# Cross-attention block in fp32: scores, G and h regrouped by quads of four tiles

## The chip, the cores and the metric

The kernel runs on one core of one Trainium2 chip. The metric is the device time of one execution in microseconds (us). All arithmetic is fp32. The engines are TensorE (matmuls; PE in the profile, its weight loads PEld), VectorE (DVE), ScalarE (ACT), GpSimd (POOL) and SyncE (SP), which issues all the DMAs here. Matmul results land in PSUM, which has eight banks of 128 partitions x 512 fp32 values.

## The reference

```python
text_p  = einsum('bld,dh->blh', x, W_text) + b_text            # x: (4, 2048, 512)
audio_p = einsum('bsd,dh->bsh', ctx_768, W_audio) + b_audio    # ctx_768: (4, 77, 384)
Q = layer_norm(text_p, g1, beta1)
K = layer_norm(audio_p, g2, beta2)
V = audio_p
alpha   = softmax(einsum('blh,bsh->bls', Q, K) / sqrt(512))    # 77 keys
H_hyper = einsum('bls,bsh->blh', alpha, V)
H_hyper = einsum('blh,hk->blk', H_hyper, W_out) + b_out
return layer_norm(H_hyper + x, g_out, beta_out)                # (4, 2048, 512)
```

## The kernel before

The 8192 rows of x are cut into 64 tiles of 128 rows, 16 tiles to each of the four batches; a group of four tiles is loaded at once. Instead of projecting x and normalising it, the kernel folds the projection into two small matrices made once in a prologue (the first 37 us). **Scores**: Q K^T is x times a 512 x 77 matrix per batch (made at L340, 78 columns with one for the offset), later scaled by 1/std of the row. **Variance**: the sum of squares of the projected row is the quadratic form x G x^T, where G = W W^T of the centred weights is a 512 x 512 matrix (made at L645). G is symmetric, so only a triangle of its 32-column blocks is kept, the off-diagonal ones doubled (`gram_out`). **Values**: V W_out + b_out is made once as `vw`, so that one matmul with softmax weights gives h.

For each tile, in order:

- `turn` (step x): VectorE transposes a 128 x 512 tile of x into `xt`, in 32 x 32 blocks; the DMA that loads `xq` has put the blocks in the right place.
- `project_chunks` (steps p and P): four matmuls, one for each 128 rows k of the contraction, with `xt[:, k]` as the 128-column stationary operand. The moving operand `mu` holds score columns and G columns side by side, in four parts of `SQ` = 20 score columns and up to 96 G columns: 464, 464, 336 and 208 columns for k = 3, 2, 1, 0 (L452). The last 128 G columns, which only k = 3 needs, don't fit the bank and go as a matmul of their own to another bank, `yl` (L460).
- `score_last` and `score` (t, s): VectorE adds the offsets to the scores, and multiplies the G product by x and sums it along the row, in two instructions (L476), one for each bank. The row sums go to `ss`.
- `row_scale` (r): GpSimd turns `ss` into 1/std. `scale_scores` (c): VectorE scales the scores and takes the row maximum. `exponential` (e): ScalarE.
- `turn_weights` (w, W): TensorE transposes a tile's 128 x 77 weights (L535), and ScalarE copies the result out of the bank (L536).
- `apply` (a): one matmul with 77 rows and 512 columns gives h (L543). `residual` (z): VectorE multiplies by 1/sum, adds x and sums the row. `squares` (q), `minus_mean` (n), `deviations` (d), `norm_shift` (o), `norm_on_scalar` (y), `norm_on_gpsimd` (m) make the last layer norm, over ScalarE and GpSimd; every fourth tile or so takes `norm_on_vector` (v, V) instead. `store` writes the tile.

The small steps (r, c, e, ...) are shared by a batch of tiles: four tiles, and two or one for the last 16 tiles (`LAST`). The order of all instructions on every engine is the program's: the first 40 tiles follow a loop with fixed distances between the steps, the rest a list written out step by step (a letter for the step, a number for the tile). `in_program_order` pins it. Every engine works its own queue in order; a DMA on SP's queue that has to wait holds up those behind it.

PSUM: banks h (two), y (two), yl0, yl1, prep, gain. In the prologue they serve as scratch; in the loop yl0 and yl1 take G's last columns and the transposed weights, prep and gain hold two constants that are read in place of SBUF (`keep`). vw is made in three blocks (L382) between the first tiles, and two of the four batches' vw are put together by DMAs.

## Time and profile before

| what | us |
|---|---|
| median of two runs | 293.35 (293.11 and 293.58) |
| span of the profiled execution | 291.9 |
| VectorE: L556 residual, L476 products of 384 and 128 columns, L403 transpose, mean of one | 0.733, 0.626, 0.353, 0.704 |
| ScalarE: L609 scale and shift, L564 squares, L523 exponential, mean of one | 0.802, 0.718, 0.349 |
| GpSimd: L613 gain, L614 shift, mean of one | 1.272, 1.271 |
| GpSimd: L506 clamp and L212 power of a four-tile batch, mean of one | 0.227, 1.037 |
| DMA: 55.33 MB in all, mean rate | 190 GB/s |

Rows of the profile name line, engine, operation, output <- inputs by tile names, shapes and count. In the lists of groups the numbers behind the bar are total busy time in us and the mean of one in ns, then the engine's idle time just before them. In a timeline a row begins with its start in us from the beginning of the span and its length; equal neighbours are merged (x2, x6). Records of matmuls overlap, since the end of one is modelled and the next starts streaming before: the distance from start to start is the cost of one, not its length.

### The profile page before, as it was taken

What the parts mean: (1) busy time and instruction counts of PE and PEld (TensorE: products, weight loads), DVE (VectorE), ACT (ScalarE), POOL (GpSimd) and SP (SyncE); (2) the same over time, 40 slices, a digit from 0 to 9 for tenths busy, and PEclk for the clock granted to TensorE, in tenths of its full rate; (3) what the DMA queues carried; (4) which work ended last, traced back from release to release, by engine and by line L of the source; (5) the groups of instructions that cost most, each with busy time, mean ns of one, the idle gap of its engine ahead of it and who ended that gap; (6) DMA issues with size and microseconds to landing.
All of it is one profiled execution on the core that took longest, in us unless ns stands there. A gap on an engine that the chain in (4) does not pass through costs nothing.

```text
span 291.9 us, 4021 instructions
## 1 busy us (share of the span) xinstructions
PE 283.0 (97%) x1034; PEld 171.6 (59%) x1034; DVE 227.1 (78%) x715; ACT 153.3 (53%) x486; POOL 157.2 (54%) x168
## 2 busy tenths in 40 slices
PE   8999999999999999999999999999999999999990
PEld 7786755565555555555555555556555556555540
DVE  1586133586878888888888989898999999989995
ACT  2646210031446383838383838366967767477571
POOL 1022000011026576757676767687989878977833
PEclk9999999999999999999999999999999999999996
DMA  6899913359390967887777878789689887612214
GB/s 200 212 267 370 214 65 99 61 183 249 92 227 36 186 245 161 274 171 263 167 265 165 269 162 270 160 274 206 262 174 294 200 270 204 159 72 88 108 58 180
DMA packets 54178, 55.33 MB, mean 190 GB/s; under 512 B 2597, under 2 KB 35697, under 8 KB 54155
## 3 DMA queue, kind: packets, MB, share of 16 engines
q1 hardware_dynamic: 54155, 55.07, 70.0%
q8 instruction: 8, 0.13, 0.2%
q14 instruction: 15, 0.12, 0.2%
HBM read 37.97 MB, written 16.78 MB: 188 GB/s over the span
## 4 chain that ended last, share of the span: by engine, by line
PE 94%; DVE 3%; issue 1%; DVEq 0%; ACT 0%
PE y L452 53%; PE h L543 18%; PE yl L460 5%; PE vw_ps L382 4%; PE m_ps L340 3%; PE vat_ps L264 3%; PE et_ps L535 2%; PE w_ps_yl L645 2%; PE w_ps_yl L208 1%; PE w_ps_y L645 1%; DVE z L595 1%; PE uw_ps L358 1%; DVE z L556 1%; DVE y L593 1%; PE va_ps L284 0%
## 5 line engine op out<-in xcount | busy, mean ns | idle before, releaser
L452 PE MATMUL y<-mu,xt 128*128 128x464 f32 (+2 forms) x512 | 179.6, 473 | 0.0
L452 PEld LDWEIGHTS y<-mu,xt 128*128 128x128 f32 x512 | 89.7, 190 | 49.6 <-issue 32.3
L543 PE MATMUL h<-vw,et 77*128 77x512 f32 x128 | 64.1, 594 | 0.1
L564 ACT ACTIVATE sqj<-z,sz 128x512 f32<-128x512 f32 x64 | 46.0, 718 | 31.9 <-DVE z L556 31.0
L613 POOL TENSOR_TENSOR z<-z,go 128x512 f32<-128x512 f32 x44 | 56.0, 1272 | 10.0 <-ACT z L609 9.4
L614 POOL TENSOR_TENSOR z<-z,beo 128x512 f32<-128x512 f32 x44 | 55.9, 1271 | 3.5
L556 DVE SCALAR_TENSOR_TENSOR z<-h,inv,x 128x512 f32<-128x512 f32 x64 | 46.5, 733 | 2.3 <-PE h L543 1.7
L403 DVE STREAM_TRANSPOSE xt<-xq 128x512 f32<-128x512 f32 x64 | 44.7, 704 | 0.5 <-PE y L452 0.5
L476 DVE CUSTOM_DVE_ANT_1 yl<-yl,x,bc 128x128 f32<-128x128 f32 x64 | 22.6, 353 | 28.2 <-PE yl L460 28.1
L476 DVE CUSTOM_DVE_ANT_1 y<-y,x,e 128x384 f32<-128x384 f32 x64 | 40.1, 626 | 2.3
L506 POOL TENSOR_SCALAR rs<-ss 128x4 f32<-128x4 f32 (+2 forms) x21 | 4.7, 223 | 66.9 <-DVE ss L476 66.6
L460 PEld LDWEIGHTS yl<-ub,xt 128*128 128x128 f32 x128 | 23.6, 188 | 26.2 <-issue 15.6
L609 ACT ACTIVATE z<-z,no,ro 128x512 f32<-128x512 f32 x44 | 34.5, 802 | 0.1
L536 ACT COPY et<-et_ps 77x256 f32<-77x256 f32 (+1 forms) x33 | 11.9, 361 | 39.5 <-PE et_ps L535 39.5
L212 POOL TENSOR_TENSOR ro<-ro,mhalf 128x4 f32<-128x4 f32 (+2 forms) x21 | 18.2, 867 | 23.7 <-ACT ro L576 23.6
L523 ACT ACTIVATE e<-e,mx 128x77 f32<-128x77 f32 x64 | 22.2, 349 | 11.9 <-DVE mx L516 11.9
L543 PEld LDWEIGHTS h<-vw,et 77*128 77x128 f32 x128 | 23.3, 190 | 7.0 <-issue 5.2
L460 PE MATMUL yl<-ub,xt 128*128 128x128 f32 x128 | 24.5, 273 | 0.0
L212 POOL TENSOR_TENSOR rs<-rs,mhalf 128x4 f32<-128x4 f32 (+2 forms) x21 | 18.6, 886 | 1.8
L498 DVE TENSOR_TENSOR e<-y,uws 128x80 f32<-128x80 f32 x64 | 15.0, 234 | 4.6 <-PE y L452 3.4
L535 PEld LDWEIGHTS et_ps<-ident,e 128*77 128x77 f32 x64 | 9.4, 147 | 15.1 <-issue 10.7
L593 DVE SCALAR_TENSOR_TENSOR y<-z,nm,gain_ps 128x512 f32<-128x512 f32 x20 | 14.9, 752 | 0.8
(107 smaller groups left out, 254.5 us busy)
## 6 DMA issues: line engine op xcount, KB each, us to landing
xq<-in_x_dram SPq DMA_DIRECT2D x64, 256.0 KB, 4.9
x<-in_x_dram SPq DMA_DIRECT2D x16, 1024.0 KB, 6.1
out_dram<-z SPq DMA_DIRECT2D x64, 256.0 KB, 2.5
wc<-in_L_xattn_W_text_dram SPq DMA_DIRECT2D x4, 256.0 KB, 5.2
wo<-in_L_xattn_W_out_dram SPq DMA_DIRECT2D x1, 1024.0 KB
wa<-in_L_xattn_W_audio_dram SPq DMA_DIRECT2D x3, 256.0 KB, 3.6
rows<-in_L_xattn_b_text_dram SPq DMA_DIRECT2D x1, 256.0 KB
bo<-in_L_xattn_b_out_dram SPq DMA_DIRECT2D x1, 256.0 KB
```

Source lines behind the costliest of these rows:

```text
L212: nc.gpsimd.tensor_tensor(dst, v, mhalf[: v.shape[0], : v.shape[1]], ALU.pow)
L403: nc.vector.transpose(xt.rearrange("p k (a j) -> p a k j", j=R), xq[i][:, t].rearrange("p a (k i) -> p a k i", i=R),)
L452: nc.tensor.matmul(parts(y[:, : Q * AQ])[:, :, cols], lhsT=xt[:, k, :], rhs=mub[:, k, :, cols], start=(k == LAST_K), stop=(k == 0),)
L460: nc.tensor.matmul(b, lhsT=xt[:, k, :], rhs=ub.rearrange("p q i -> p (q i)"), start=True, stop=True)
L476: nc.vector.tensor_tensor_reduce(out=y, in0=y, in1=x, scale=1.0, scalar=first, op0=ALU.mult, op1=ALU.add, accum_out=to)
L523: nc.scalar.activation(e, e, AF.Exp, bias=s.mx[:, c], accum_out=s.inv[:, c])
L543: nc.tensor.matmul(s.h[n], lhsT=s.et[:, n - s.tiles[0], :], rhs=s.vw, start=True, stop=True)
L556: nc.vector.scalar_tensor_tensor(z, s.h.pop(n), s.inv[:, c], xs[i][:, t, :], ALU.mult, ALU.add, accum_out=s.sz[:, c])
L564: nc.scalar.activation(junk, s.z[n], AF.Square, bias=s.sz[:, c], scale=-float(H), accum_out=s.sq[:, c])
L609: nc.scalar.activation(z, z, AF.Identity, bias=s.no[:, c], scale=s.ro[:, c])
L613: nc.gpsimd.tensor_tensor(z, z, go, ALU.mult)
L614: nc.gpsimd.tensor_tensor(z, z, beo, ALU.add)
```

## The change

Tiles are handled by quads of four (14 quads, then batches of 2, 2, 2, 1 and 1 tiles).

- **G fills a bank** (`form`, step G): the moving operand is G alone, 512, 384, 256 and 128 columns for k = 3 to 0, in one y bank; `form_sum` (s) is one VectorE instruction over 512 columns. yl's own matmul is gone.
- **Scores in their own bank** (`score`, step S): four matmuls of 78 columns for each tile, with the same stationary operands as G; the four tiles of a quad share one bank (yl0 and yl1 by turns). `offsets` (A) adds the offsets of a whole quad in one instruction.
- **Keys in three pieces**: `exponential` writes the 77 weights of a row (padded to 96 with zeros) as three pieces of 32, the pieces of the four tiles side by side; so a transpose of 128 x 128 (three for a quad) puts the four tiles' weights on the four groups of 32 partitions.
- **h of four tiles in row groups of 32 rows** (`apply_four`, step H): for each piece four matmuls, one per tile, each with 32 rows (13 in the last piece) of its own group of partitions, 512 columns, to four different banks (h, h, prep, gain), accumulated over the three pieces. vw is made by pieces too (W, U) and copied by 19 DMAs to all four groups of partitions; the last eight tiles keep the matmul of 77 rows.
- The transposed weights use the scores' bank; `keep` keeps one constant, late. `deviations` is split into two steps (d, D), `norm_on_gpsimd` into m and M, `norm_shift` goes from ScalarE to VectorE. 57 tiles end on GpSimd, 7 on VectorE. The loop is replaced by a list of steps for all tiles; matmuls that only kept TensorE warm near the end are gone.

```diff
-    soft = ctx.enter_context(tc.tile_pool(name="soft", bufs=4))
+    soft = ctx.enter_context(tc.tile_pool(name="soft", bufs=2))
...
-    SQ = -(-(S + 1) // Q)
-    S1 = Q * SQ
-    LAST_K = ND - 1
-    AQ = SQ + LAST_K * R
-    assert Q == ND and Q * AQ <= 4 * P
-
+    S1 = Q * -(-(S + 1) // Q)
+    NP = -(-S // R)
+    assert Q == ND == T and T * S1 <= 4 * P and NP < 4
...
-    mu = [const.tile([P, ND, Q, AQ], F32, name=f"mu_{i}") for i in range(2)]
-    ub = const.tile([P, Q, R], F32, name="ub")
+    gr = const.tile([P, ND, Q, P], F32, name="gr")
+    ms = const.tile([P, ND, B, S1], F32, name="ms")
+    e2 = [const.tile([P, T, NP * R], F32, name=f"e2_{i}") for i in range(2)]
+    for t in e2:
+        nc.gpsimd.memset(t[:, :, S:], -1e30)
...
-        for b in range(2):
-            (nc.vector.tensor_copy if b else nc.scalar.copy)(
-                mu[b][:, k, :, :SQ], parts(pm[:, b, :])
-            )
-        nc.scalar.copy(later[:, k], pm[:, 2:, :])
+        (nc.vector.tensor_copy if k % 2 else nc.scalar.copy)(ms[:, k], pm)
...
+        nc.vector.tensor_copy(uws[:, :, 0, S], bc2.to_broadcast([P, B]))
...
+    vwq = [batch.tile([P, NP, H], F32, name=f"vwq_{b}") for b in range(B)]
+    vwl = batch.tile([S, H], F32, name="vwl")
...
+    def values_by_piece(p):
+        keys = vat[:, :, p * R : p * R + N].rearrange("p j (b s) -> p j b s", s=S)
+        t = zs.tile([P, H], F32, name=f"vap_{p}", tag="z")
+        vap.append(t.rearrange("p (j b i) -> p j b i", j=NH, b=B))
+        nc.gpsimd.tensor_copy(vap[p], keys[:, :, :, :R])
+
+    def value_weights(p):
+
+        pvw[p] = flat(bank("h", f"vw_ps_{p}"))
+        for j in range(NH):
+            nc.tensor.matmul(
+                pvw[p],
+                lhsT=vap[p][:, j].rearrange("p b i -> p (b i)"),
+                rhs=wo[:, j, :],
+                start=(j == 0),
+                stop=(j == NH - 1),
+            )
+
+    def value_weights_out(p):
+        nc.vector.tensor_tensor(vwa[:, p], pvw.pop(p), bo, ALU.add)
+        if p < NP - 1:
+            return
+        for b in range(B):
+            for r in range(Q):
+                nc.sync.dma_start(
+                    out=vwq[b][r * R : (r + 1) * R], in_=vwa[b * R : (b + 1) * R]
                 )
...
+        for p in range(NP):
+            z = min(S, (p + 1) * R)
+            nc.sync.dma_start(
+                out=vwl[p * R : z], in_=vwa[(B - 1) * R : (B - 1) * R + z - p * R, p]
+            )
...
-    LAST = [2, 2, 2, 2, 2, 2, 2, 1, 1]
+    LAST = [2, 2, 2, 1, 1]
+    QUADS = (NT - sum(LAST)) // T
     batches, start = [], 0
-    for size in [T] * ((NT - sum(LAST)) // T) + LAST:
+    for size in [T] * QUADS + LAST:
...
+            self.b = groups[f // T][0]
+            self.uw = uws[:, self.b]
+            self.quad = self.m == T
+            i = batches.index(tiles)
+            self.e = e2[i % 2]
+            self.ps = bank(f"yl{i % 2}", f"s_{f}")
+            self.s = flat(self.ps)[:, : T * S1].rearrange("p (t s) -> p t s", s=S1)
...
-    def project_chunks(n, ks):
-        mub = made[groups[n // T][0]][0]
-        xt = turned[n]
-        y, b = ys[n]
-        for k in ks:
-            cols = slice(0, SQ + min(k + 1, LAST_K) * R)
+    def score(n):
+
+        s, _ = of(n)
+        for k in range(ND):
             nc.tensor.matmul(
-                parts(y[:, : Q * AQ])[:, :, cols],
-                lhsT=xt[:, k, :],
-                rhs=mub[:, k, :, cols],
-                start=(k == LAST_K),
+                s.s[:, n - s.tiles[0], : S + 1],
+                lhsT=turned[n][:, k, :],
+                rhs=ms[:, k, s.b, : S + 1],
+                start=(k == 0),
+                stop=(k == ND - 1),
+            )
+        del turned[n]
+
+    def form(n):
+
+
+        slot_begins(n)
+        ys[n] = flat(bank("y", f"y_{n}"))
+        for k in reversed(range(ND)):
+            cols = slice(0, (k + 1) * R)
+            nc.tensor.matmul(
+                parts(ys[n])[:, :, cols],
+                lhsT=turned[n][:, k, :],
+                rhs=gr[:, k, :, cols],
+                start=(k == ND - 1),
                 stop=(k == 0),
             )
-            if k == LAST_K:
-                nc.tensor.matmul(
-                    b, lhsT=xt[:, k, :], rhs=ub.rearrange("p q i -> p (q i)"), start=True, stop=True
-                )
-
-    def begin_project(n):
-
-        begun[0] = n
-        slot_begins(n)
-        ys[n] = flat(bank("y", f"y_{n}")), flat(bank(f"yl{n % 2}", f"yl_{n}"))[:, :P]
-        project_chunks(n, (3, 2))
-
-    def end_project(n):
-        project_chunks(n, (1, 0))
-        del turned[n]
-
-    def sum_of_products(y, x, first, to):
-        nc.vector.tensor_tensor_reduce(
-            out=y, in0=y, in1=x, scale=1.0, scalar=first, op0=ALU.mult, op1=ALU.add, accum_out=to
-        )
-
-    def score_last(n):
+
+    def form_sum(n):
 
 
         i, t = divmod(n, T)
         s, c = of(n)
-        yl = parts(ys[n][1])
-        sum_of_products(
-            yl, parts(xs[i][:, t, :])[:, :, LAST_K * R :], bc2, s.uw[:, 0, S : S + 1]
...
+        y = ys.pop(n)
+        nc.vector.scalar_tensor_tensor(
+            y, y, 1.0, xs[i][:, t, :], ALU.mult, ALU.mult, accum_out=s.ss[:, c]
+        )
+
+    def offsets(f):
+
+        s = state[f]
+        e = s.s[:, : s.m, : S + 1]
+        nc.vector.tensor_tensor(
+            e, e, s.uw[:, 0, : S + 1].unsqueeze(1).to_broadcast([P, s.m, S + 1]), ALU.add
+        )
+        ss = s.ss[:, : s.m]
+        nc.vector.tensor_tensor(ss, ss, s.s[:, : s.m, S], ALU.add)
...
     def exponential(f):
-        s = state[f]
+
+
+        s = state[f]
+        if s.quad:
+            s.ex = soft.tile([P, NP, T, R], F32, name=f"ex_{f}", tag="ex")
         for q in range(s.m):
             c = slice(q, q + 1)
-            e = s.e[:, q, :S]
-            nc.scalar.activation(e, e, AF.Exp, bias=s.mx[:, c], accum_out=s.inv[:, c])
-
-    def turn_weights(f, a=0):
-
-
-        s = state[f]
-        z = a + min(s.m, 2) if s.m == T else s.m
-        if a == 0:
-            s.et = soft.tile([S, T, P], F32, name=f"et_{f}", tag="et")
-
-        pe = bank(f"yl{(begun[0] + 1) % 2}", f"et_ps_{f}_{a}")
-        for q in range(a, z):
-            nc.tensor.transpose(pe[:S, q, :], s.e[:, q, :S], ident)
-        nc.scalar.copy(s.et[:, a:z, :], pe[:S, a:z, :])
+            if s.quad:
+                e, ex = s.e[:, q, :].rearrange("p (a i) -> p a i", i=R), s.ex[:, :, q, :]
+            else:
+                e = ex = s.e[:, q, :S]
+            nc.scalar.activation(ex, e, AF.Exp, bias=s.mx[:, c], accum_out=s.inv[:, c])
+
+    def turn_weights(f):
+
+        s = state[f]
+        if s.quad:
+            for p in range(NP):
+                nc.tensor.transpose(s.ps[:, p, :], s.ex[:, p].rearrange("p t i -> p (t i)"), ident)
+        else:
+            for q in range(s.m):
+                nc.tensor.transpose(s.ps[:S, q, :], s.e[:, q, :S], ident)
+
+    def keep_weights(f):
+        s = state[f]
+        s.et = soft.tile([P, NP, P], F32, name=f"et_{f}", tag="et")
+        n, m = (P, NP) if s.quad else (S, s.m)
+        nc.scalar.copy(s.et[:n, :m, :], s.ps[:n, :m, :])
+
+    def apply_four(f):
+
+
+        s = state[f]
+        for t, tag in enumerate(("h", "h", "prep", "gain")):
+            s.h[f + t] = flat(bank(tag, f"h_{f + t}"))
+        for p in range(NP):
+            n = min(R, S - p * R)
+            for t in range(T):
+                rows = slice(t * R, t * R + n)
+                nc.tensor.matmul(
+                    s.h[f + t],
+                    lhsT=s.et[rows, p, :],
+                    rhs=vwq[s.b][rows, p, :],
+                    start=(p == 0),
+                    stop=(p == NP - 1),
+                )
...
-            s.h[n], lhsT=s.et[:, n - s.tiles[0], :], rhs=s.vw, start=True, stop=True
+            s.h[n], lhsT=s.et[:S, n - s.tiles[0], :], rhs=vwl, start=True, stop=True
...
-    def norm_on_vector(n, step):
+    def norm_on_vector(n):
 
 
         s, c = of(n)
         z = s.z[n]
-        if step == 0:
-            y = scored_y[-2 if any(b is scored_y[-1] for b in in_bank.values()) else -1]
-            in_bank[n] = y
-            nc.vector.scalar_tensor_tensor(y, z, s.nm[:, c], kept[1] if kept else go, ALU.add, ALU.mult)
-        else:
-            nc.vector.scalar_tensor_tensor(z, in_bank.pop(n), s.ro[:, c], beo, ALU.mult, ALU.add)
-            store(n)
+        y = flat(bank("prep", f"no_ps_{n}"))
+        nc.vector.scalar_tensor_tensor(y, z, s.nm[:, c], kept[0], ALU.add, ALU.mult)
+        nc.vector.scalar_tensor_tensor(z, y, s.ro[:, c], beo, ALU.mult, ALU.add)
+        store(n)
 
     def norm_shift(f):
 
         s = state[f]
         s.no = small.tile([P, T], F32, name=f"no_{f}", tag="no")
-        for q in range(s.m):
-            c = slice(q, q + 1)
-            nc.scalar.mul(s.no[:, c], s.nm[:, c], s.ro[:, c])
+        nc.vector.scalar_tensor_tensor(
+            s.no[:, : s.m], s.sz[:, : s.m], -1.0 / H, s.ro[:, : s.m], ALU.mult, ALU.mult
+        )
...
-    def norm_on_gpsimd(n):
+    def gain_on_gpsimd(n):
         z = of(n)[0].z[n]
         nc.gpsimd.tensor_tensor(z, z, go, ALU.mult)
+
+    def shift_on_gpsimd(n):
+        z = of(n)[0].z[n]
         nc.gpsimd.tensor_tensor(z, z, beo, ALU.add)
         store(n)
...
     for step in """
...
+        G16 m5 z8 e12 S16 M5 z9 G17 s16 m6 q8 i12 z10 q9 M6 S17 x19 G18 q10 s17 m7 z11 x20 q11 M7
+        S18 s18 w12 d8 G19 D8 k12 x21 o8 y8 S19 y9 s19 m8 H12 y10 A16 M8 x22 y11 r16 G20 z12 m9 c16
...
     """.split():
```

## The prediction

> **What bounds the kernel now.** The page was read first for the engine that never stops, then for the chain that ends last.
>
> ```profile
> PE 283.0 (97%) x1034; PEld 171.6 (59%) x1034; DVE 227.1 (78%) x715; ACT 153.3 (53%) x486; POOL 157.2 (54%) x168
> ...
> PE   8999999999999999999999999999999999999990
> ...
> PEclk9999999999999999999999999999999999999996
> ...
> PE 94%; DVE 3%; issue 1%; DVEq 0%; ACT 0%
> PE y L452 53%; PE h L543 18%; PE yl L460 5%; PE vw_ps L382 4%; PE m_ps L340 3%; PE vat_ps L264 3%; PE et_ps L535 2%; PE w_ps_yl L645 2%; PE w_ps_yl L208 1%; PE w_ps_y L645 1%; DVE z L595 1%; PE uw_ps L358 1%; DVE z L556 1%; DVE y L593 1%; PE va_ps L284 0%
> ```
>
> TensorE is the bound, at full clock, and the chain of waits is a chain of matmuls. So the change is priced on TensorE: busy time alone says little there, start-to-start times say it all. The timeline of TensorE in mid-kernel gives them:
>
> ```profile
> 123.39 0.38 PE L460 MATMUL yl<-ub,xt 128*128 128x128 f32 x2
> 123.61 1.86 PE L452 MATMUL y<-mu,xt 128*128 128x464 f32 x6
> 125.31 1.02 PE L543 MATMUL h<-vw,et 77*128 77x512 f32 x2
> 126.17 0.38 PE L535 MATMUL et_ps<-ident,e 128*77 128x128 f32 x2
> 126.39 0.94 PE L452 MATMUL y<-mu,xt 128*128 128x464 f32 x2
> 127.17 0.38 PE L460 MATMUL yl<-ub,xt 128*128 128x128 f32 x2
> ```
>
> Each fp32 matmul of the code is two records here: two passes, each with its own weight load. From start to start, six y passes take 1.70 us, two more 0.78, two yl 0.22, the two passes of one h 0.86 (0.43 each, 0.84 ns per moving column), two one-pass transposes 0.22. A tile thus pays 1.70 + 0.78 + 0.22 = 2.70 us for G and scores, 0.86 for h, 0.11 for its transpose. Check: 64 x 3.67 = 234.9, and three vw blocks of 8 passes (8 x 0.43 = 3.44) make 10.3, together 245.2; TensorE's stretch from the first y (37.2 us) to the last tiles' h (about 282) is 244.8. There is no stall in it to win back.
>
> The third view is the timeline around two stretches of short passes, one of weight loads and one of their matmuls, then two groups by shape.
>
> ```profile
> 8.50 0.64 PEld L264 LDWEIGHTS vat_ps<-cat,wa 128*128 128x128 f32 x5
> ...
> 8.48 0.72 PE L264 MATMUL vat_ps<-cat,wa 128*128 128x103 f32 x5
> ...
> 19.59 0.43 PE L246 MATMUL kt_ps<-ident,kn 77*128 77x77 f32 x4
> 19.86 1.50 PE L645 MATMUL w_ps_yl<-wct 128*128 128x384 f32 x4
> ...
> L452 PEld LDWEIGHTS y<-mu,xt 128*128 128x128 f32 x512 | 89.7, 190 | 49.6 <-issue 32.3 <-PE y L452 2.2 <-DVE z L595 1.2
> ...
> L246 PEld LDWEIGHTS kt_ps<-ident,kn 77*128 77x128 f32 x4 | 0.4, 140 | 0.1
> ```
>
> Passes of 103 columns should stream in 103 x 0.84 = 87 ns. They run at (0.72 - 0.28) / 4 = 0.110 us (0.28 is the mean of one record), and their loads of 128 columns at (0.64 - 0.19) / 4 = 0.1125. So a pass with a fresh 128-column fp32 load costs at least about 0.111 us, however few columns it moves. The one row below that is the transposes, (19.86 - 19.59) / 4 = 0.068 us at 77 columns, and their loads are of another kind (140 ns against 190).
>
> **G and scores.** Before, the 20 score columns of each quarter rode in the same passes as G. After, G is 512 + 384 + 256 + 128 = 1280 columns in two passes: 2 x 1280 x 0.84 ns = 2.15 us. Scores are four matmuls of 78 columns with 128-column weights, 8 passes. By columns they would take 8 x 78 x 0.84 ns = 0.52, and the tile's 1592 columns against 1600 would be a wash. By the load they take 8 x 0.111 = 0.89. Ends: 0.52 (streaming) and 0.89; I take 0.89, since the 103-column rows have the same instruction, load and type. Sum 3.04 against 2.70: +0.34 us a tile, 64 tiles, **+21.8 us**. All of it lies on the path.
>
> **h in row groups.** Fourteen quads replace four h (4 x 0.86 = 3.44 us) by 12 matmuls of at most 32 rows, still 512 columns and two passes: 24 passes, 24 loads. No row shows matmuls on different row groups, so the cost has two ends. Full overlap: the pieces would stream in 3 x 0.86 = 2.58, but 24 loads at 0.111 make 2.66. No overlap: 24 x 0.43 = 10.32. Between them stands the order: every pair of passes in the timeline is first pass, second pass of one matmul, and each starts when the stream before it ends. If starts keep that order, a matmul's second pass must wait for its first on the same rows, and holds back the next group's first pass, which can overlap only that second pass: one 0.43 step per matmul, 12 + 1 steps, 5.59 us. I take this, since no row shows a later pass overtaking one that waits. Quad: 5.59 - 3.44 = +2.15, three transposes instead of four -0.11, so 14 x 2.04 = **+28.6 us**. Should a group's load not be pulled ahead of the waiting pass, each step is 0.43 + 0.111, 12 x 0.541 + 0.43 = 6.92 a quad, +18.6 more.
>
> The Trainium skill, "TensorE: Matmul & The Clock Gate", Part 3 (Packing small matmuls), says that four row tiles of 32 rows and 512 columns gave 3.07 times the speed, and also that matmuls start and end strictly in program order. No run here shows either. By the first, 24 x 0.43 / 3.07 = 3.36 us a quad would make the whole change about +19 us (312 us); the second speaks for the sum that I take. The page "TensorEngine Tiling (Array Packing)", Key Properties, adds that a change of tiling mode drains the engine.
>
> Entering and leaving a group may also wait for the end of a running pass: a 512-column record lasts 0.59 us with starts 0.43 apart, so 0 to 0.16, 28 times, 0 to 4.5; half, **+2.2 us**, as no row is nearer to either end.
>
> **The rest, at nothing.** vw stays at 24 passes of 0.43. VectorE loses the 80-column add and the two products and gets one 512-column product (like the 733 + 84 ns of L556) and a 312-column add per quad: 4 x (704 + 817 + 817 + 291) ns + about 1.5 us = 12 us a quad, beside at least 15 of TensorE. GpSimd now has all four tiles of a quad: 8 x 1.272 + 0.23 + 1.04 + 1.02 = 12.5 us; ScalarE some 10. Cover gone only if TensorE fell to 12.5 a quad, which no case below does. Added waits: scaling a quad (VectorE) waits for GpSimd's rsqrt, itself behind a shift of 1.27 us, with the next G product behind it; two y banks let TensorE go on for 3.04 us and more. The four h need the banks of the last quad's residuals, done some steps before. The piece-wise vw needs 19 transfers (3.2 MB; at the page's 190 GB/s some 17 us) between its last add and the first grouped h, five tiles or 15 us later, the first batch's quarter first: 0; without that cover at most one landing of about 5 us. On SP's queue they stand ahead of x loads that are needed two groups later: 0. The prologue loses GpSimd and ScalarE copies that the score matmuls covered, and gains three GpSimd copies early: 0, within 1. The tail after the last G is the same chain of about 13 us (the last y passes end at 278.6): 0, within 2.
>
> **Sum.** 21.8 + 28.6 + 2.2 = +52.6. On the profiled 291.9 us that is 344.5; the median lies 1.45 us above the span (launch and end around it), so **346 us**.
>
> **Rivals.** (a) *The groups overlap fully.* h costs 2.66, a quad saves 0.78 + 0.11, 14 quads 12.4; with the scores +9.4, with drains up to 13.9: 303 to 307. For it: nothing in the code links the groups, they write different banks. Against: the order of passes. (b) *The row groups do not overlap at all*, so that the change is not what it says: 10.32 a quad, +94.8 + 21.8, 410 us. Only unrelated single matmuls with few rows are in the trace. (c) *Faster:* the scores' loads hide, so that a 78-column pass takes the 0.068 us of the transposes, and the groups overlap fully: 9.4 - 64 x 8 x 0.043 = -12.6, 281 us. It decides from a pass of 0.111 - 9.4 / 512 = 0.093 us down. For it: the transposes' 0.068; against: the 103-column rows, five in a run with the same load.
>
> **How the numbers follow.** Steps in order 0.50 (344 to 367 us); full overlap or something near the middle 0.31 (303 to 325); no overlap 0.06; faster 0.08; within 2% (full overlap with a score pass of about 0.09 us) 0.05. Range 302 to 362: it leaves out (b), the faster and equal cases and the top of the likeliest, some 2 in 10. What a measurement can tell from no change is about 2%, 5.9 us; the two runs lie 0.47 apart. Faster 0.08, same 0.05, slower 0.87.
>
> **What would show it.** In the profile after: score passes 0.11 us apart with loads back to back; y passes 0.43, 0.32, 0.21, 0.11; 24 h passes of a quad over 5.6 us (2.7 in (a), 10.3 in (b)); quads 18 us apart instead of 14.7; TensorE still 97%. I am wrong in the scores if their passes come at 0.07, in h if the group lasts under 3.5 us, and in the cover if VectorE or GpSimd ends TensorE's waits.

## Result, and the profile after

The changed kernel takes 316.62 us (median of two runs, 315.43 and 317.80) against 293.35. The ratio of its runs to those of the kernel before is 1.080, with a 95% interval of 1.070 to 1.090. The forecast was slower, 346 us, in a range of 302 to 362. So the direction and the range held, but the loss is 23.3 us where 52.6 were forecast. The profiled execution has a span of 315.9 us, 24.0 more than before. (Of the runs below one is left out of its kernel's figures, the profiled run of e1, which took 392.88 us at a granted clock of 0.84.)

The page of the changed kernel, in the lines that answer to those shown of before (engines, TensorE's busy tenths and granted clock, the chain that ended last, two groups):

```profile
PE 298.6 (95%) x1619; PEld 202.6 (64%) x1619; DVE 198.6 (63%) x548; ACT 147.6 (47%) x398; POOL 186.7 (59%) x188
...
PE   8999789999999999999999999999999999999840
...
PEclk9999979999999999999999999999999999999975
...
PE 94%; DVE 4%; ACT 1%; issue 0%; DVEq 0%
...
L466 PEld LDWEIGHTS s<-ms,xt 128*128 128x128 f32 x512 | 62.9, 193 | 2.2 <-issue 1.5
...
L415 DVE STREAM_TRANSPOSE xt<-xq 128x512 f32<-128x512 f32 x66 | 46.2, 703 | 6.4 <-DMA xq<-in_x_dram 4.2
```

TensorE is still the bound and still never waits in the middle. VectorE has lost 28.5 us of busy time and GpSimd has gained 29.5, and the chain hardly shows either (DVE 4%, POOL none). Three things are new. There are 585 more matmul records. TensorE's tenths sag in the fifth and sixth of the 40 slices (32 to 47 us) and at the end, and so does its clock in the sixth and the last two. And VectorE makes 66 transposes, two more than there are tiles.

The timeline of TensorE in mid-kernel is the view that prices the steps, from start to start:

```profile
147.89 2.36 PE L482 MATMUL y<-gr,xt 128*128 128x512 f32 x8
150.09 1.01 PE L466 MATMUL s<-ms,xt 128*128 128x78 f32 x8
150.94 0.49 PE L544 MATMUL s<-ident,ex 128*128 128x128 f32 x3
151.27 2.32 PE L482 MATMUL y<-gr,xt 128*128 128x512 f32 x8
153.43 1.01 PE L466 MATMUL s<-ms,xt 128*128 128x78 f32 x8
154.37 2.86 PE L565 MATMUL h<-vwq,et 32*128 32x512 f32 x24
157.16 2.42 PE L482 MATMUL y<-gr,xt 128*128 128x512 f32 x8
...
169.81 2.86 PE L565 MATMUL h<-vwq,et 32*128 32x512 f32 x24
```

G takes 2.20 us a tile, the scores 0.85 (8 passes 0.106 apart), three transposes 0.33, and the 24 passes of a grouped h 2.79. From one grouped h to the next it is 15.43 us, against 14.68 for four tiles before. The scores just ahead of the grouped h take 0.94, 0.09 more than the others, and the G behind it takes 2.26 (to the next scores at 159.42), 0.06 more: entering and leaving the group cost 0.15 to 0.2 us, an estimate from these rows; 0.2 is used below.

How the row groups run shows in the windows of the same 24 passes (columns: stretch, length, TensorE busy and the matmuls that touch the stretch, weight loads likewise, clock, DMA):

```profile
154.37:154.40 0.03, 0.03 (x4) 0.03 (x4) 1.00 0.97 137
154.40:154.90 0.50, 0.50 (x4) 0.28 (x8) 1.00 1.13 212
154.90:155.33 0.43, 0.43 (x8) 0.20 (x4) 1.00 0.90 317
```

and in the timeline of the weight loads:

```profile
154.37 0.31 PEld L565 LDWEIGHTS h<-vwq,et 32*128 32x128 f32 x8
```

In the first 0.03 us four matmuls and four loads have begun: the first passes of four different matmuls start some 7 ns apart, each on its own row group. Eight loads are done after 0.31 us, so the next four passes, which start 0.53 us after the first, find their weights loaded. Then four passes start in each 0.43 us, with the loads one step ahead. Six steps of four, not thirteen of one or two.

The sag at 40 us is in the timeline of all engines around the first tile:

```profile
39.61 1.89 DVE L415 STREAM_TRANSPOSE xt<-xq 128x512 f32<-128x512 f32 x3
...
40.37 3.86 PE L482 MATMUL y<-gr,xt 128*128 128x512 f32 x8 [2.96 <-DVE xt L415]
```

The prologue still turns tiles 0 and 1 (L761 and L762), and the new list begins with x0 x1 x2: both tiles are turned twice, and the second time stands on VectorE's queue behind the copies of `score_offsets`. TensorE waits 2.96 us for it, and in the first G behind the wait (40.37 to 44.02 us) the granted clock is 0.61. The first G starts at 40.37 us instead of 37.21, takes 3.65 us instead of 2.16, and the scores behind it 1.14 instead of 0.85: 3.16 + 1.49 + 0.29 = 4.9 us.

**Where the 24.0 us lie.** Head 4.9. Fourteen quads at 15.43 instead of 14.68, 0.76 each in the mean of all: 10.6. The last eight tiles, which have the separate scores and the old h, 8 x 0.33 = 2.7. The end, from the last pass on scores (before: on G and scores) to the end, 16.4 instead of 13.3: 3.1. The rest is 2.7. Of it 1.7 are two h (0.86 each) that stood behind the last such pass before and now stand ahead of it: four h follow it in the kernel before, two in the changed one. Another 0.46 is a wait of TensorE for ScalarE's copy of the weights; the last 0.5 was not traced.

### The profile page after: what moved, and what is told of

Same layout as the page of the kernel before. It is cut to its first block, busy times and chain, and to the rows that moved or that the text cites. A ratio compares the mean times of both kernels' runs of the same rounds, so it can differ in the third digit from the quotient of the medians.

```text
span 315.9 us, 4937 instructions
## 1 busy us (share of the span) xinstructions
PE 298.6 (95%) x1619; PEld 202.6 (64%) x1619; DVE 198.6 (63%) x548; ACT 147.6 (47%) x398; POOL 186.7 (59%) x188
## 4 chain that ended last, share of the span: by engine, by line
PE 94%; DVE 4%; ACT 1%; issue 0%; DVEq 0%
PE y L482 45%; PE s L466 17%; PE h L565 12%; PE vw_ps L384 3%; PE m_ps L340 3%; PE vat_ps L264 2%; PE h L577 2%; PE w_ps_yl L681 2%; PE s L544 1%; DVE z L628 1%; PE w_ps_yl L205 1%; DVE no_ps L627 1%; PE w_ps_y L681 1%; DVE z L590 1%; PE uw_ps L354 1%; PE va_ps L284 0%
## 5 line engine op out<-in xcount | busy, mean ns | idle before, releaser
L482 PE MATMUL y<-gr,xt 128*128 128x512 f32 (+3 forms) x512 | 152.8, 442 | 3.0 <-DVE xt L415 3.0
L482 PEld LDWEIGHTS y<-gr,xt 128*128 128x128 f32 x512 | 93.3, 192 | 66.7 <-issue 42.1
L646 POOL TENSOR_TENSOR z<-z,go 128x512 f32<-128x512 f32 x57 | 72.6, 1274 | 22.0 <-ACT z L642 22.0
L496 DVE SCALAR_TENSOR_TENSOR y<-y,x 128x512 f32<-128x512 f32 x64 | 44.7, 699 | 53.8 <-PE y L482 53.6
L650 POOL TENSOR_TENSOR z<-z,beo 128x512 f32<-128x512 f32 x57 | 72.5, 1271 | 3.6
L466 PE MATMUL s<-ms,xt 128*128 128x78 f32 x512 | 65.3, 271 | 0.0
L466 PEld LDWEIGHTS s<-ms,xt 128*128 128x128 f32 x512 | 62.9, 193 | 2.2 <-issue 1.5
L537 ACT ACTIVATE ex<-e,mx 128x96 f32<-128x96 f32 x56 | 20.3, 364 | 59.6 <-DVE mx L523 59.6
L565 PE MATMUL h<-vwq,et 32*128 32x512 f32 (+1 forms) x336 | 40.0, 605 | 0.0
L209 POOL TENSOR_TENSOR ro<-ro,mhalf 128x4 f32<-128x4 f32 (+2 forms) x19 | 17.5, 919 | 17.4 <-DMA xq<-in_x_dram 8.7
L565 PEld LDWEIGHTS h<-vwq,et 32*128 32x128 f32 (+1 forms) x336 | 15.9, 184 | 13.7 <-issue 12.6
```

The lines of the kernel that those rows point to most:

```text
L209: nc.gpsimd.tensor_tensor(dst, v, mhalf[: v.shape[0], : v.shape[1]], ALU.pow)
L466: nc.tensor.matmul(s.s[:, n - s.tiles[0], : S + 1], lhsT=turned[n][:, k, :], rhs=ms[:, k, s.b, : S + 1], start=(k == 0), stop=(k == ND - 1),)
L482: nc.tensor.matmul(parts(ys[n])[:, :, cols], lhsT=turned[n][:, k, :], rhs=gr[:, k, :, cols], start=(k == ND - 1), stop=(k == 0),)
L496: nc.vector.scalar_tensor_tensor(y, y, 1.0, xs[i][:, t, :], ALU.mult, ALU.mult, accum_out=s.ss[:, c])
L565: nc.tensor.matmul(s.h[f + t], lhsT=s.et[rows, p, :], rhs=vwq[s.b][rows, p, :], start=(p == 0), stop=(p == NP - 1),)
L646: nc.gpsimd.tensor_tensor(z, z, go, ALU.mult)
```

## The experiments

**e1: the two tiles turned once.**

```diff
-        x0 x1 x2 G0 S0 s0 W0 x3 G1 U0 S1 s1 W1 x4 G2 U1 S2 s2 W2 x5 G3 U2 S3 s3 G4 A0 x6 r0 S4 s4
+        x2 G0 S0 s0 W0 x3 G1 U0 S1 s1 W1 x4 G2 U1 S2 s2 W2 x5 G3 U2 S3 s3 G4 A0 x6 r0 S4 s4
```

> The list of steps begins with the transposes of tiles 0 and 1, which the prologue has already made; here the second ones are left out. If they cause the late start (first G pass at 40.37 us instead of 37.21) and the slow clock behind it (first G 3.65 us instead of 2.16, first scores 1.13 instead of 0.85): 3.16 + 1.50 + 0.28 = 4.9 us less, 311.7 us, first G pass near 37.3. Rival: something else is late there too (score copies, pieces of V, a bank): the wait moves, 315 us or more.

Measured: 312.12 us (median of three runs, 312.02 to 313.67), ratio 1.065 (1.062 to 1.069). That is 4.5 us less than the changed kernel, of the 4.9 expected, where the two runs of the changed kernel lie 2.4 apart. In e5, which has the same edit, the timeline of TensorE shows the first G where it belongs and at full speed, with the scores behind it at 39.05:

```profile
36.89 2.32 PE L482 MATMUL y<-gr,xt 128*128 128x512 f32 x8
```

The first grouped h of e5 starts at 71.94 us instead of 77.20. So the head is shown, within a microsecond.

**e2: h by four matmuls of 77 rows.** With it the transposes go back to four of 77 columns, and vw is copied once per batch; all else is as in the change.

```diff
-                    lhsT=s.et[rows, p, :],
-                    rhs=vwq[s.b][rows, p, :],
...
+        for t in range(T):
+            nc.tensor.matmul(
+                s.h[f + t], lhsT=s.et[:S, t, :], rhs=vwl[s.b], start=True, stop=True
+            )
```

> The grouped h is undone alone: four matmuls of 77 rows at the same place, four transposes of 77 columns, V W_out copied once per batch of rows. If the groups overlap fully and a quad pays 2.79 us plus about 0.20 for entering and leaving, against 3.44 plus one transpose (0.11) here: +0.56 us a quad, 14 quads, +7.9, 324.5 us. Rival, the groups' gain is given back elsewhere (waits for four banks, 19 copies): 316.6, within 1 us. In the order of the prediction (5.59 a quad) it would be 30 us faster, 287.

Measured: 326.03 us, ratio 1.111 (1.108 to 1.114). The old h starts every 16.04 us in its timeline, 0.61 later than the grouped one:

```profile
141.33 3.64 PE L557 MATMUL h<-vwl,et 77*128 77x512 f32 x8
...
157.37 1.06 PE L557 MATMUL h<-vwl,et 77*128 77x512 f32 x2
```

So the grouping, which the forecast made the larger loss (+28.6), is a gain of 9.4 us (326.03 - 316.62), and what is left of the change makes the kernel slower: the scores for the most part, with the head and the end.

**e3: the two loops of the grouped h swapped**, so that all three pieces of a tile stand before those of the next.

```diff
-        for p in range(NP):
-            for t in range(T):
+        for t in range(T):
+            for p in range(NP):
```

> The two loops of the grouped h change places: all six passes of one tile, then those of the next, so neighbours share a row group. If each row group works through its own passes and waiting ones are overtaken from far behind: 2.79 us a quad as before, 316.6 us, within 2. If a pass overtakes only its near neighbours: the four tiles overlap at their borders alone, 24 passes less 3 overlaps at 0.43 = 9.0 us a quad, +6.2 x 14 = +87, 404 us. In between: a look-ahead of limited depth, with its depth to be read from the starts.

Measured: 361.25 us, ratio 1.231 (1.228 to 1.235): between the two. The windows of its grouped h, cut where a tile's first pass starts:

```profile
149.96:150.93 0.97, 0.97 (x4) 0.48 (x5) 1.00 1.22 190
150.93:151.90 0.97, 0.97 (x8) 0.70 (x8) 1.00 0.61 201
```

Each tile starts 0.97 us after the one before, when that one's third pass of six starts; the group takes 5.67 us instead of 2.79. A tile's six passes follow each other on one row group, so starts in program order would have held the next tile back until the sixth had started. It passed three that were waiting, and no more. In the change's own order the fourth group's first pass has just three second passes to overtake. Whether the limit lies in the passes or in their weight loads is not shown. 14 x 2.88 = 40 us of the 44.6 more than the change; 3.4 of the rest are two quads of 20.01 us instead of 18.32, in which the granted clock was 0.91 in the mean.

**e4: three of a tile's four score matmuls with 39 columns instead of 78.** This leaves out, for keys 39 to 76 and the offset's column, the part of the sum over contraction rows 128 to 511.

```diff
-                s.s[:, n - s.tiles[0], : S + 1],
+                s.s[:, n - s.tiles[0], : 39 if k else S + 1],
```

> Three of the four score matmuls of each tile move 39 columns instead of 78 (for keys 39 to 76 and the offset column the sum over rows 128 to 511 of the contraction is left out). If a pass is bound by its weight load of 128 columns (0.107 us): no change, 316.6 within 0.7. If by its columns (0.84 ns each): 6 x 39 x 0.84 ns x 64 = 12.6 us less, 304 us.

Measured: 316.94 us, ratio 1.080 (1.078 to 1.082): nothing is won by moving half the columns. A tile's scores take 0.81 us instead of 0.85, and the G behind them 0.04 more. In its groups the loads are as many and as long as in the change:

```profile
L466 PEld LDWEIGHTS s<-ms,xt 128*128 128x128 f32 x512 | 62.7, 192 | 2.2 <-issue 1.5
L466 PE MATMUL s<-ms,xt 128*128 128x39 f32 (+1 forms) x512 | 63.1, 271 | 0.0
```

So a score pass is not bound by its columns: with a fresh 128-column load it costs 0.10 to 0.11 us, at 39 columns as at 78. In both kernels the loads are busy through all of a tile's scores (0.85 of 0.85 us, 0.81 of 0.81), which makes them the likely bound.

**e5: e1, and the last tile's scores earlier, with seven and two transposes that keep TensorE busy near the end.**

```diff
-        e60 A62 z59 q58 i60 r62 v52 w60 n58 M55 k60 q59 a60 s63 m56 d58 a61 c62 z60 e62 S63 D58 w62
-        i62 q60 A63 M56 o58 z61 k62 y59 a62 v53 r63 n60 q61 m57 c63 d60 z62 e63 D60 w63 i63 M57 n62
+        e60 A62 z59 q58 i60 r62 v52 w60 n58 M55 k60 S63 q59 a60 s63 A63 r63 m56 d58 a61 c62 z60 e62 D58 w62
+        i62 q60 M56 o58 z61 k62 y59 a62 v53 n60 q61 m57 c63 d60 z62 e63 D60 X7 w63 i63 X2 M57 n62
```

> On top of the transposes made once, the end is changed: the scores of tile 63 are issued before the h of tiles 60 and 61 (1.72 us earlier on TensorE) with their offsets and scaling next to them, and nine transposes of the identity keep TensorE's clock up before and after the last weights' transpose. If the longer tail (16.4 us from the last score pass to the end, against 13.3 from the last G pass before) comes from the late scores and the last h at a lower clock (2.09 us against 0.86): 1.2 us for the clock and 1 to 1.7 for the order less, 309.5 to 310.5. Rival: VectorE's last norms set the end: 312.5, no change.

A miss: 314.58 us, ratio 1.073 (1.071 to 1.075), 2.5 more than e1. TensorE still stood idle 3.2 us before the last transposes, and the last h still took 2.08 us. What sets the changed kernel's end is not shown. In its trace the chain behind the last scores is VectorE's for some 10 us and TensorE's for 2.1, the last h; VectorE is busy 11.4 of the 16.4 us, against 10.0 of 13.3 before. In e5 the chain also has GpSimd in it.

**The grouped h alone.** If it gains and the scores lose, the kernel before with nothing but the grouped h should beat both. It needs four banks for h, so prep and gain no longer keep constants. Eight kernels test that.

**e6:** keys in pieces, `apply_four` and the 19 copies put into the kernel before, with its order.

```diff
+        for t, tag in enumerate(("h", "h", "prep", "gain")):
+            s.h[f + t] = flat(bank(tag, f"h_{f + t}"))
...
-        vws[i] = (vw[i] if i < 2 else prep.tile([P, H], F32, name=f"vws_{i}"))[:n]
...
+                    out=vwq[b][r * R : (r + 1) * R], in_=vwa[b * R : (b + 1) * R]
```

> The kernel before with the grouped h alone: scores stay in G's passes, 12 quads get three transposes and the h of four tiles in row groups, the rest as before; the constants in PSUM give their banks to h. If the groups are worth what the trace shows (a quad 2.79 + 0.20 + 0.33 against 3.43 + 0.44): 12 x 0.55 = 6.6 us less than before, 286.8 us, and the change lost by its scores alone. Rival: in this order the copy of a quad's weights or the banks make TensorE wait, and the gain is gone: 293 us or more.

349.75 us, ratio 1.192 (1.190 to 1.194). The grouped h itself is nearly as quick as in the change (2.86 us as one row of the timeline, 2.93 in some quads), and the rest waits. Its timeline of TensorE:

```profile
143.60 0.55 PE L560 MATMUL et_ps<-ident,ex 128*128 128x128 f32 x3 [3.21 <-ACT ex L551]
```

All four exponentials must now be done before the first transpose, and in e6 that costs 3.2 us in most quads, 29.5 in all.

**e7: e6 with the steps behind the scores one tile later, and the copies one batch at a time.**

```diff
-        run({1: [("w", 5)], 2: [("a", 6)]}.get(t, []), n)
+        run({2: [("w", 6)], 3: [("a", 7)]}.get(t, []), n)
```

> The kernel before with the grouped h, mended where the last run made TensorE wait (up to 4.6 us once for tiles of x whose loads stood behind 19 copies on SP's queue, 2.2 us in every quad for the exponentials of all four tiles): the copies of V W_out go out by batches of rows, and a quad's transposes, its h and all steps behind them come one tile later. If those waits were all that ate the gain: 293.3 - 12 x 0.55 = 286.7 us. If VectorE, now at 83% of the body's time, has become the bound in this order: 290 us or more.

330.85 us, ratio 1.127 (1.125 to 1.130). The grouped h now stopped halfway for some 2.4 us (1.3 to 1.5 shown as a wait for a residual of the last quad, whose bank it needs).

**e8: e7 with the residuals of a quad in three tiles, and all tiles of the loop on GpSimd.**

```diff
-        run([("i", 8)] * (t == 0) + [("z", 8)], n)
+        zq = {0: [8], 1: [8, 7], 2: [7], 3: []}[t]
+        run([("i", 8)] * (t == 0) + [("z", a) for a in zq], n)
```

> As the last run, with h's banks freed sooner: there each grouped h stood still for about 2 us in the middle until VectorE had read the last h of the quad before. Now a quad's four residuals come in three tiles' time, all tiles of the loop end on GpSimd (the norm on VectorE took 1.6 us instead of 0.75 with its constant in SBUF), and a tile's store is put two tiles later on SP's queue. If only the banks, the queue and VectorE's order held the gain back: a quad at 14.1 us instead of 14.7, 287 us. If the four banks leave too little room beside this VectorE load: 293 us or more.

A miss again: 326.13 us, ratio 1.111 (1.104 to 1.117). Its quads are 16.67 us apart, with two waits in each, this one and 0.64 us at the last columns of G for ScalarE's copy of the weights:

```profile
159.24 1.02 PE L477 MATMUL y<-mu,xt 128*128 128x464 f32 x2 [1.42 <-DVE ss L501]
```

**e9: the residuals one to a tile, the scaling of the scores beside the grouped h, where VectorE stood idle, all that follows four tiles later; the transposed weights in a bank of h.**

```diff
-        zq = {0: [8], 1: [8, 7], 2: [7], 3: []}[t]
-        run([("i", 8)] * (t == 0) + [("z", a) for a in zq], n)
-        if t == 0:
-            run([("c", 4)], n)
-        run({2: [("w", 6)], 3: [("a", 7)]}.get(t, []), n)
+        run([("i", 12)] * (t == 0) + [("z", 12)], n)
+        run({2: [("w", 10)], 3: [("c", 7), ("a", 11)]}.get(t, []), n)
```

> As e8 (the kernel before with the grouped h alone), with the waits that e8's timeline still shows taken apart: the residuals of a quad one to a tile instead of three in two tiles, the scaling of a quad's scores moved beside the grouped h (VectorE stands idle there for 3.0 us), all steps after it four tiles later, and the transposed weights in a bank of h, so that yl no longer waits for their copy. Theory (the grouped h is worth about 0.55 us a quad in the old order too, and e6 to e8 lost it to waits of 2.1 us a quad on VectorE and ScalarE): the quads from 11 to 39 run 14.1 us apart against 14.66 before and 16.67 in e8, TensorE's waits there under 0.3 us a quad; the whole 290 to 300 us, the end of the list (tiles 40 to 43, where four residuals more have to be made up) being worth some us. Rival (the grouped h needs VectorE and GpSimd in bursts that the two y banks cannot cover, so that the new order with scores of their own is the only way to it): quads still over 15 us apart, 315 us or more.

Half right. The whole was 319.88 us, ratio 1.090 (1.086 to 1.095), but the loop stood as the theory said, in TensorE's timeline:

```profile
136.06 2.93 PE L579 MATMUL h<-vwq,et 32*128 32x512 f32 x24
...
150.24 2.94 PE L579 MATMUL h<-vwq,et 32*128 32x512 f32 x24
```

Quads are 14.17 us apart without a wait, 0.51 under the kernel before. After tile 40, where the four tiles of lag had to be made up, TensorE stood idle some 24 us, the longest time 10.3.

**e10: the lag of e8 again, the scores scaled one or two tiles at a time, and a list from tile 40 on laid out by each engine's sum.** Near the end it writes a pair's scaled scores over those of the pair before while they are still to be transposed, so some of the last tiles have other weights; the instructions are the same.

```diff
-        if t == 0:
-            run([("c", 4)], n)
+        run({0: [("c", 4)], 1: [("c", 4), ("c", 3)], 2: [("c", 3)]}.get(t, []), n)
```

> The kernel before with the grouped h alone, with e9's even steps also behind tile 40, where e9's TensorE stood idle 23 us (the four tiles that its steps lagged more had to be made up). The residuals again lag 8 to 11 tiles and one falls on each tile, scores are scaled one or two tiles at a time, 13 quads are grouped, and the steps from tile 40 on are laid out so that each engine's sum fits: by the mean durations of e8 and e9, VectorE and GpSimd then have some 100 us each for the rest, TensorE 91. Theory (e9's loop stands at 14.17 us a quad without a wait; the whole is then set by VectorE and GpSimd at the end): quads in the loop 14.1 to 14.4 us apart, the whole 286 to 293 us, just under or at the kernel before. Rival (scaling beside the residuals cannot be kept off the two y banks, as in e8): quads over 15 us apart, 300 us or more.

The rival's number: 340.05 us, ratio 1.157 (1.154 to 1.161), quads 17.5 us apart. What it brought to light is the price of a scaling. This is what the trace says of that line in e9, with the shortest, the median and the longest time in ns:

```profile
L537 DVE SCALAR_TENSOR_TENSOR e<-e,rs,uws x64: 257/296/1319, 67.6 to 307.2; 128x77 f32<-128x77 f32 x64
```

and of the same step in the kernel before, first with the constant in PSUM (`w_ps`), then with both operands in SBUF, in the time when GpSimd had little to do (busy 1.3 of the 13.7 us):

```profile
L513 DVE SCALAR_TENSOR_TENSOR e<-e,rs,w_ps x56: 253/293/297, 88.7 to 281.6; 128x77 f32<-128x77 f32 x56
L513 DVE SCALAR_TENSOR_TENSOR e<-e,rs,uws x8: 293/298/301, 60.9 to 74.6; 128x77 f32<-128x77 f32 x8
```

The median is the same; with two SBUF operands some scalings last as long as one gain or shift on GpSimd (1.27 us), and the mean is 0.62 in e8, 0.70 in e9 and 0.78 in e10. The timeline of e10 has a long one beside a shift:

```profile
147.75 1.27 POOL L670 TENSOR_TENSOR z<-z,beo 128x512 f32<-128x512 f32 x1
147.96 1.17 DVE L537 SCALAR_TENSOR_TENSOR e<-e,rs,uws 128x77 f32<-128x77 f32 x1
```

The scaling starts while the shift runs, and ends 0.11 us after it; the one before, 0.61 us long, ends 0.10 after a gain.

**e11: about e8's distances, the residuals one to a tile, with that constant back in PSUM.** The last columns of G of two tiles share one bank, the other keeps the offsets; a new list from tile 40 on.

```diff
-        ys[n] = flat(bank("y", f"y_{n}")), flat(bank(f"yl{n % 2}", f"yl_{n}"))[:, :P]
+        ys[n] = flat(bank("y", f"y_{n}")), ylp[:, n % 2]
...
-                s.x[:, q, :S], s.e[:, q, :S], s.rs[:, q : q + 1], s.uw[:, 1, :S], ALU.mult, ALU.add
+                s.x[:, q, :S], s.e[:, q, :S], s.rs[:, q : q + 1], wps[:, s.b, :S], ALU.mult, ALU.add
```

> The kernel before with the grouped h alone, with one constant back in PSUM: in the kernel before, the scaling of the scores reads its offset from bank prep and takes 0.291 us a tile (L513, 56 times); in e6 to e10 banks prep and gain belong to the grouped h, the scaling reads two operands in SBUF and takes 0.68 to 0.70 us in the mean, but 0.297 in the 8 of the kernel before that ran while GpSimd was still idle. Here the last columns of G of two tiles share bank yl0, and yl1 keeps the offsets; the transposed weights use a bank of h. Residuals lag 8 to 11 tiles, one to a tile, a quad's scores are scaled together, as in e8; the steps from tile 40 on are laid out anew so that each engine's sum fits. Theory (it was this 0.4 us a tile on VectorE that filled e8's and e10's queue): the scaling back at 0.29 to 0.35 us, the quads in the loop 14.1 to 14.3 us apart against 16.67 in e8, 17.5 in e10 and 14.66 before; the whole 286 to 294 us, by the layout's own sum 182 + 103 + 2 = 287 for the span. Rival (the burst of scaling and residuals on VectorE is too long for two y banks whatever it reads): quads over 15.5 us, the whole over 305 us.

308.23 us, ratio 1.049 (1.046 to 1.052). The scaling was back at 0.29 us and the waits for VectorE were gone from the loop. One wait was left, 1.41 us a quad, for ScalarE's copy of the transposed weights: quads 15.65 us apart, over the rival's mark, for a cause that neither theory had. The constant's return is not tested by itself: the order differs from e8's and e10's too, and e9's loop ran without a wait while its scalings took 0.70 in the mean. Shown is what a scaling costs, not what share of those waits it made.

**e12: the transposes one tile earlier, and a new list from tile 40 on, with pairs to the end.** The copy was moved with them, but also still issued at its old place.

```diff
-        run([("p", 0), ("s", 1), ("t", 0)] + [("w", 7)] * (t == 3) + [("P", 0)], n)
-        run([("o", 12)] * (t == 0) + [("y", 12)], n)
+        run([("p", 0), ("s", 1), ("t", 0)] + [("w", 6)] * (t == 2) + [("P", 0)], n)
+        run([("W", 6)] * (t == 2) + [("o", 12)] * (t == 0) + [("y", 12)], n)
```

> As e11, with the transposes of the weights one tile earlier, so that ScalarE's copy of them is done when the grouped h comes up: that copy was the only wait of TensorE left in e11's loop, 1.41 us in each of eight quads, 11.3 in all. The steps from tile 40 on are laid out anew by the durations that e11 showed (two latencies after TensorE and ScalarE were too short), with pairs to the end. Theory (the grouped h is worth 0.5 us a quad in the old order once VectorE and ScalarE keep up, and the rest is the layout's end): quads in the loop 14.1 to 14.3 us apart without a wait, 12 of them grouped, worth some 6 us against the kernel before; the end after tile 40 costs part of that: 290 to 298 us. Rival (another wait of about 1 us a quad takes the place of the copy, on the residuals or the row sums): quads over 15 us, over 302 us.

306.27 us, ratio 1.043 (1.040 to 1.046): the same wait, 11.3 us in all, now for the second copy.

**e13: the copy once.**

```diff
-        run({0: [("e", 4)], 3: [("W", 7), ("a", 7), ("n", 11), ("d", 11), ("D", 11)]}.get(t, []), n)
+        run({0: [("e", 4)], 3: [("a", 7), ("n", 11), ("d", 11), ("D", 11)]}.get(t, []), n)
```

> As e12, which still issued the copy of the transposed weights a second time at its old place, so that the 1.41 us a quad stayed; here the copy is issued once, right behind the transposes. Theory (the grouped h is worth 0.5 us a quad in the old order once the queues of VectorE and ScalarE keep up): quads of the loop 14.1 to 14.4 us apart, the wait of 11.3 us gone and nothing in its place, so 306.3 - 11.3 = 295 us, 293 to 297, the same as the kernel before within 2%; what 12 quads gain (6 us) the end behind the last G gives back (19 us from the last score pass to the end in e12 against 13.3 before). Rival (another wait takes its place): over 300 us.

295.91 us, ratio 1.009 (1.007 to 1.010). The line that scales, and TensorE's timeline:

```profile
L537 DVE SCALAR_TENSOR_TENSOR e<-e,rs,w_ps_kept x64: 265/290/296, 60.7 to 276.7; 128x77 f32<-128x77 f32 x64
```

```profile
126.50 3.05 PE L583 MATMUL h<-vwq,et 32*128 32x512 f32 x24
...
140.85 3.04 PE L583 MATMUL h<-vwq,et 32*128 32x512 f32 x24
```

The longest scaling is 296 ns, the quads are 14.35 us apart, 0.33 under the kernel before, and TensorE waits nowhere in the loop. The last pass on G ends at 273.9 us, 4.7 before that of the kernel before (278.6). But 1.7 of that are two h that now stand behind it (six, before four), and the end behind it takes 19.2 us instead of 13.3: the gain is gone. The windows from 182 us on and behind the last G, first in e13, then in the kernel before (busy time of TensorE, its loads, VectorE, ScalarE, GpSimd):

```profile
182.00:293.00 111.00, 97.25 (x407) 56.09 (x405) 96.01 (x293) 68.98 (x218) 85.43 (x85) 0.96 0.66 186
273.90:293.10 19.20, 6.84 (x22) 3.06 (x21) 14.86 (x33) 9.08 (x30) 11.23 (x12) 0.77 0.35 137
```

```profile
182.00:291.90 109.90, 102.28 (x362) 59.62 (x361) 97.53 (x301) 70.51 (x224) 84.70 (x88) 0.98 0.64 180
278.63:291.90 13.27, 5.65 (x20) 2.30 (x19) 10.01 (x26) 6.13 (x22) 5.03 (x7) 0.81 0.31 119
```

From 182 us on VectorE and GpSimd have as much to do as before, within 2 us, and TensorE 5 us less. Behind the last G, VectorE has 14.9 us of work left instead of 10.0, and GpSimd 11.2 instead of 5.0. So TensorE comes to its end sooner, and the others' work does not. No version tried beats the kernel before; whether a better list for the last tiles would is open.

## Why the prediction was right and wrong

**Scores and G: right.** Predicted 3.04 us a tile against 2.70, +21.8 in all. Measured: a quad's 15.43 less its h (2.79), the 0.20 around it and its transposes (0.33) leaves 12.11, 3.03 a tile, +0.33, or 21.1 us for 64. The choice between streaming (0.52) and loads (0.89) was right (0.85, or 0.81 with half the columns), and e4 shows that the columns are not the bound, not only the size.

**h in row groups: the step that failed.** It read "If starts keep that order, a matmul's second pass must wait for its first on the same rows, and holds back the next group's first pass". They do not keep it: four first passes start within 0.03 us, past the waiting second passes. (The description of the kernel says that every engine works its own queue in order; for passes on different row groups TensorE does not.) 2.79 us a quad instead of 5.59, so with the transposes -0.76 a quad and -10.6 us over 14 quads in place of +28.6. That is 39 us, more than the whole miss of 29; the terms put at nothing, 10.7 together, stand against it. The premise came from rows that show no passes on different row groups; they could not speak for such passes. Rival (a) had the overlap, but its 2.66 a quad lies near 2.79 by luck: it was 24 loads one after the other, and the trace shows four loads in 0.20 us and six steps of 0.43 us.

The Trainium skill, "TensorE: Matmul & The Clock Gate", Part 3, holds that matmuls keep strict program order in start and end, and gives 3.07 times the speed for four row tiles of 32 rows and 512 columns. Here 24 passes of 0.43 take 2.79 us, 3.7 times, and e3 shows that later matmuls start before earlier ones that wait. The measurement decides: between row groups passes overtake up to three that wait, in these two kernels.

**Mode switches:** predicted 2.2, estimated from the rows after at 14 x 0.15 to 0.20, so 2.1 to 2.8. Right in size; that a running pass has to end is not shown.

**Head and end: at nothing, and wrong.** The head was "0, within 1" and cost 4.9: the list of steps was not read against the prologue, which had already turned two tiles. The end was "0, within 2" and takes 3.1 more, with two h fewer in it; these two h (1.7), a wait of 0.46 and 0.5 that was not traced stand ahead of it. Why it is longer is open.

**Cover: right for the change.** VectorE, GpSimd and SP's 19 copies never held TensorE up between 61 and 262 us.

In sum: 21.1 - 10.6 + 2.8 + 4.9 + 3.1 + 1.7 + 0.5 = 23.5 of the 24.0. Rival (a) stood at 302.8 (291.9 + 9.4 + 1.45) before drains; with the measured 2.8 and 4.9, and 5.8 for the end and what stands ahead of it, it would have been 316.3. It had the smaller chance, and its price left out head and end. That the time fell into the stated range owes nothing to the case held likeliest (344 to 367): the range reached down to 302 for rival (a).

## What to carry to other kernels

Rows that all use the same resource say nothing about work on different ones: where the trace shows no case of two row groups, the order of starts is as unknown as the overlap, and should be priced at both ends. Here a matmul of few columns with its own 128-column fp32 load cost 0.11 us a pass, so splitting it off another matmul lost even though the columns balanced. And a bank that a change takes away was used for something: here, without its constant in PSUM, a scaling on VectorE went from 0.29 us to 0.62 to 0.78 in the mean. Last, a gain on TensorE counts only if the other engines' work ends sooner too; in e13 it did not.

## What was not expected of the hardware

Row groups overtake each other, but not far: 2.79 us with the tiles in the inner loop, 5.67 with them in the outer one, for the same 24 passes (e3).

A VectorE instruction with both operands in SBUF can last as long as the GpSimd instruction beside it: 0.26 to 1.32 us for the same scaling in e9, 0.27 to 0.30 in e13 with one operand in PSUM. The Trainium skill, "SBUF — State Buffer", section "SBUF: two separate sides", says that VectorE and GpSimd share a pair of ports under an exclusive lock, which also a VectorE instruction with two SBUF inputs takes against a GpSimd instruction that reads SBUF; these numbers, and the ends 0.10 and 0.11 us after GpSimd's in e10, agree with it.

A wait of TensorE costs more than itself: after the 2.96 us in the head the granted clock was 0.61 over the first G, which took 3.65 us, and without the wait, in e5, it took 2.16. The clock also fell without a wait: in e3 it was 0.50 from 211 to 214 us, with TensorE busy throughout; why is open.
